# Layer 3 of a four-layer graph kernel: distances once per unordered pair of column blocks, looped by columns

## The chip, the cores and the metric

The kernel runs on one core of a Trainium2 chip. A core has five engines with a queue each, all in order: TensorE (PE in the profile, its weight loads PEld), VectorE (DVE), ScalarE (ACT), GpSimd (POOL) and SyncE (SP, which here issues the transfers). They meet only at semaphores. SBUF is the working memory with 128 partitions; PSUM takes TensorE's results. The metric is the device time of one execution in microseconds; the median of several runs is compared.

## The reference

3327 nodes with 64 features, a dense adjacency matrix of 3327 x 3327 with about 0.2% of its entries set, four layers. Each is `x = x + layer(relu(layernorm(x)), adj)`: two gated graph convolutions, a hyperbolic convolution, a convolution with weights by rank, and the layer that is changed here, a hyperbolic attention:

```python
x_tan = _logmap0(x, C)
left = x_tan @ att_W[:D] + att_b
right = x_tan @ att_W[D:]
adj_att = jax.nn.sigmoid(left + right.T) * adj
x_local = _logmap(x[:, None, :], x[None, :, :], C)
support_t = jnp.einsum('ij,ijd->id', adj_att, x_local)
return _proj(_expmap(x, support_t, C), C)
```

For each pair of nodes (i, j), `_logmap` needs a distance of the two and a factor that depends on this distance alone. Distance and factor are the same for (i, j) and (j, i). The attention is not: sigmoid(left_i + right_j) and adj[i, j] belong to the ordered pair. The sum over j gives, for each i, 64 features and one more number.

## The kernel before, in words

The nodes are padded to 3328 = 26 blocks of 128. Blocks b and b + 13 form a *column*, so there are 13 columns with two halves each. Columns 0 to 5 are group 0 (`gs_`, 768 node columns per half), columns 6 to 12 group 1 (`gf`, 896). Targets i lie along the free axis, sources j on the partitions. A program written in Python emits the instructions; `manual_schedule` leaves them in the order in which they are emitted, so that order is each engine's queue. `Weave` holds generators of other work; each `weave.tick()` emits the next step of those that are due.

Layers 0 to 2 stream the adjacency matrix several times. Layer 3 begins at about 455 us. Its nodes' own quantities come from `nodes3`: for group 1 during layer 2, for group 0 (`gen_s`) woven into layer 3's first steps. It yields some 25 times, with layer norm, transposes, bf16 rows of per-node terms (`rows_i`, `rows_j`), and `leftb`, the left terms spread over all partitions.

The loop before runs over 26 `pairs`: target group 1 with all 13 source columns, then target group 0 with all 13. Step n does for a source column c, with its halves b and the targets' halves k:

- `distances` (L1239, L1251): four products of 64 rows in fp32 and four in bf16 for each k, into PSUM `pair(0)` for b = 0 and `pair(1)` for b = 1. A Gelu (L1259) out of each stands for the logarithm-like factor, a long Tanh (L1266) for the sigmoid.
- `squares` (L1282, L1283 on ScalarE, L1284 on VectorE): the Gelu's result is squared with an offset.
- `weights` (L1294): (tanh + 1) times an adjacency tile, on VectorE.
- `products3` (L1303): (square + HD) times this weight, on VectorE.
- `gather` (L1315): for each half, 64 feature rows accumulated in PSUM banks 2 and 3, the two target halves in the two column halves of the array. `gather_p` (L1332): one more row, with 32-column weights `p2c` whose first column is filled, four products side by side, in bank 0.

Three steps are in work at a time: products of n, attention of n + 1, first distances of n + 2. Tiles of the adjacency come through `Stream`: four slots in layer 3, a load as soon as a slot is free, SyncE's queue (L287), one tile of 128 x 1792 or 128 x 1536 for each half of each step, 52 in all.

After step 12, `collected` for group 1 evicts the accumulators, transposes them, and runs `finish` (L1143 to L1216: some forty small and eight large VectorE instructions, two square roots' worth of table loads on ScalarE, the store); it is woven into the next steps. After step 25 the same follows for group 0 with nothing beside it. A general path behind a branch (`ok < 1`) isn't taken with these inputs.

Of the kernel before, what the change touches and what calls it, by code (L numbers as in the profile page):

```python
# [124 lines left out]

def uses_of_tiles():

    last_first = [2 * c + h for c in reversed(range(HB)) for h in range(2)]
    layer3 = [(g, k) for g in (1, 0) for k in F_SRC + S_SRC]
    starts, uses = [], []  # L130
    for u in (
        FIRST + SECOND + THIRD + LAYER1,
        [(1, k) for k in last_first],
        [(0, k) for k in last_first],
        layer3,
    ):
        starts.append(len(uses))
        uses += u
    return uses, starts[1:]
# [70 lines left out]
def gnn_kernel(ctx: ExitStack, tc: tile.TileContext, t, out):  # L210
# [51 lines left out]
    loaded = [0]  # L262

# [17 lines left out]
    def load_tile(s, key):  # L281
        sum_edges(stream.slots[s][1])
        g, k = key
        pool = slots_a if s < SLOTS3 else slots_b if s < SLOTS2 else slots_c
        a = pool.tile([P, WIDE], F32, name="adj", tag=f"adj{s}")
        a = a[:, : 2 * GROUPS[g].w]
        nc.sync.dma_start(a, t[f"adj{g}"][k * P : (k + 1) * P, :])  # L287
        loaded[0] += 1
        if loaded[0] in between:
            between[loaded[0]]()  # L290
        return a
# [29 lines left out]
    diff = p0.tile([P, P], I32, name="diff")  # L321
    G.iota(diff, pattern=[[1, P]], base=0, channel_multiplier=-1)
    eye, tri, rest, identb = (p0.tile([P, P], BF16, name=n) for n in ("eye", "tri", "rest", "identb"))
# [525 lines left out]

    def by_halves(a):  # L850
        return a.rearrange("p (c a) -> p a c", a=2)

    def nodes3(g, m_t):
# [110 lines left out]
        V.tensor_scalar(p2c[:, sl, 0], qv, 2.0, 2.0, op0=OP.mult, op1=OP.add)  # L964
# [17 lines left out]
    with ExitStack() as c2:  # L982
# [10 lines left out]
        def mask(n):  # L993

            if n < len(work):
                a = stream.tile(stream.now)
                w = 2 * GROUPS[work[n][0]].w
                masks[n] = mk.tile([P, WIDE], BF16, name="mask", tag=f"mask{n % 5}")
# [76 lines left out]
        for n in range(WL):  # L1075
            weights(n)
        for n in range(2):
# [5 lines left out]
        for n in range(len(work)):  # L1083
# [25 lines left out]
            p2c = n3f.tile([P, NB, 32], F32, name="p2c")  # L1109
# [110 lines left out]
    with ExitStack() as cf:  # L1220
        wk = cf.enter_context(right("wkf"))

        pairs = [(i, c) for i in (1, 0) for s in (gf, gs_) for c in s.cs]
        gl, ths, adjs, acc = {}, {}, {}, {}

        def begin(n):
            gl[n] = [wk.tile([P, WIDE], F32, name="gl", tag=f"gl{b}", bufs=3) for b in range(2)]
            ths[n] = [wk.tile([P, WIDE], F32, name="th", tag=f"th{b}", bufs=2) for b in range(2)]

        def distances(n, k):  # L1230

            i, c = pairs[n]
            g = GROUPS[i]
            pts = [pair(b) for b in range(2)]
            for lo, hi in g.chunks:
                for b in range(2):
                    rs = slice(b * D, (b + 1) * D)
                    rhs = (xs, xw)[(k + b) % 2]
                    T.matmul(  # L1239
                        pts[b][:, P + lo : P + hi],  # L1240
                        lhsT=xs[rs, c * P : (c + 1) * P],
                        rhs=rhs[rs, g.c0 * P + lo : g.c0 * P + hi],
                        start=True,
                        stop=False,
                    )
                s = gf if c >= gf.c0 else gs_
                for b in range(2):
                    rs = slice(b * D, (b + 1) * D)
                    j0 = s.off + b * s.w + (c - s.c0) * P
                    i0 = g.off + k * g.w  # L1250
                    T.matmul(  # L1251
                        pts[b][:, P + lo : P + hi],
                        lhsT=rows_j[rs, j0 : j0 + P],
                        rhs=rows_i[rs, i0 + lo : i0 + hi],
                        start=False,
                        stop=True,
                    )
            for b in range(2):
                S.activation(  # L1259
                    gl[n][b][:, k * g.w : (k + 1) * g.w],  # L1260
                    pts[b][:, P : P + g.w],
                    AF.Gelu,
                    scale=-HA,
                )
            kk = 2 * c + k
            S.activation(  # L1266
                ths[n][k][:, : 2 * g.w],
                leftb[:, g.off : g.off + 2 * g.w],
                AF.Tanh,
                bias=righth[:, kk : kk + 1],  # L1270
# [3 lines left out]
        def split(g):  # L1274

            return g.w // 2 + 64, 2 * g.w

        def squares(n):

            m, w = split(GROUPS[pairs[n][0]])  # L1280
            a, b = gl[n]
            S.activation(a[:, :w], a[:, :w], AF.Square, bias=hg)  # L1282
            S.activation(b[:, :m], b[:, :m], AF.Square, bias=hg)  # L1283
            V.scalar_tensor_tensor(  # L1284
                b[:, m:w], b[:, m:w], 2 * HG, b[:, m:w], op0=OP.add, op1=OP.mult
            )

        def weights(n):

            i, c = pairs[n]  # L1290
            for b in range(2):
                a = stream.tile(stream.now)
                th = ths[n][b][:, : 2 * GROUPS[i].w]
                V.scalar_tensor_tensor(th, th, 1.0, a, op0=OP.add, op1=OP.mult)  # L1294
                stream.done()

        def products3(n):

            m, w = split(GROUPS[pairs[n][0]])
            th = ths.pop(n)  # L1300
            for b, lo, hi, hd in ((0, 0, w, HD), (1, 0, m, HD), (1, m, w, HD + HG * HG)):
                a = gl[n][b][:, lo:hi]
                V.scalar_tensor_tensor(a, a, hd, th[b][:, lo:hi], op0=OP.add, op1=OP.mult)  # L1303

        def gather(n):
            i, c = pairs[n]
            g = GROUPS[i]
            if n % HB == 0:
                acc["x"] = accumulators((2, 3))
                acc["p"] = bank(0)  # L1310
            for b in range(2):
                first, last = n % HB == 0 and b == 0, n % HB == HB - 1 and b == 1
                for q, (lo, hi) in enumerate(g.chunks):
                    for k in range(2):
                        T.matmul(  # L1315
                            acc["x"][q][k * D : (k + 1) * D, : hi - lo],
                            lhsT=xd[:, 2 * c + b, :],
                            rhs=gl[n][b][:, k * g.w + lo : k * g.w + hi],
                            start=first,
                            stop=last,  # L1320
                        )

        def gather_p(n):
            i, c = pairs[n]
            g = GROUPS[i]
            a = gl.pop(n)
            for b in range(2):
                first, last = n % HB == 0 and b == 0, n % HB == HB - 1 and b == 1
                for q, (lo, hi) in enumerate(g.chunks):
                    for k in range(2):  # L1330
                        r = 32 * (2 * q + k)
                        T.matmul(  # L1332
                            acc["p"][r : r + 32, : hi - lo],
                            lhsT=p2c[:, 2 * c + b, :],
                            rhs=a[b][:, k * g.w + lo : k * g.w + hi],
                            start=first,
                            stop=last,
                        )

        def evict(g):  # L1340
            m, pp = flat(big(g, "h_n")), flat(big(g, "xc"))
            for q, (lo, hi) in enumerate(g.chunks):
                if q:
                    S.activation(m[:, lo:hi], acc["x"][q][:, : hi - lo], AF.Copy)
                else:
                    V.tensor_copy(m[:, lo:hi], acc["x"][q][:, : hi - lo])
            m0, m1 = (hi - lo for lo, hi in g.chunks)
            V.tensor_copy(pp[:, :m0], acc["p"][:, :m0])
            if m1 > m0:
                S.activation(pp[D:, m0:m1], acc["p"][D:, m0:m1], AF.Copy)  # L1350
            return m, pp

        def collected(g, m, pp):
            yield
            n0, n1 = ((hi - lo) // P for lo, hi in g.chunks)
            ((p, _, _),) = pieces(1)
            for i in range(n1):
                r = 0 if i < n0 else D
                T.transpose(
                    p[:, i * P + r : (i + 1) * P],  # L1360
                    pp[r:, i * P : (i + 1) * P],
                    ident[r:, r:],
                )

            v = p[:, : n1 * P].rearrange("p (i q a r) -> p i q a r", q=2, a=2, r=32)
            for q, n in enumerate((n0, n1)):
                sl = slice(2 * q * n0, 2 * q * n0 + 2 * n)
                V.tensor_mul(
                    sums[:, g.slots, D][:, sl].rearrange("p (i a) -> p i a", a=2),
                    v[:, :n, q, :, 0],  # L1370
                    qs[:, g.slots][:, sl].rearrange("p (i a) -> p i a", a=2),
                )
# [21 lines left out]
        final = None  # L1394


        for n in range(-2, len(pairs)):
# [305 lines left out]
```

## Time and profile before

| | us |
|---|---|
| median of 3 runs | 762.37 (760.78 to 762.52) |
| the profiled execution | 764.75 |
| its span, first to last instruction | 762.9 |
| mean granted TensorE clock in it | 0.950 |
| TensorE busy (share of the span) | 651.7 (85%) |
| VectorE busy | 500.2 (66%) |
| ScalarE busy | 420.7 (55%) |
| GpSimd busy | 5.8 (1%) |
| layer 3's loop, first Gelu to last gather | 455.5 to 740.8 |

The profile is one execution, taken by the hardware profiler. A group's row gives line, engine, operation, tiles, shapes and count, then its busy time, the mean duration of one, and the idle time of its engine just before. The timeline gives start, duration, engine, line and count of neighbouring instructions of one kind; the duration of several is from the first's start to the last's end. Durations overlap where an engine works as a pipeline, so the price of one in a series is the distance between starts. Table rows by stage give the busy time of each engine in a window, then the clock granted to TensorE (1.00 is full), the share of DMA engines in use, and GB/s. The ends of TensorE's products are modelled.

### The profile page before, as it was taken

To read this page: it belongs to the slowest core of one execution; us is meant where nothing else is said; L and a number is where in the kernel's file an instruction comes from. 1 tells how busy PE (TensorE), PEld (TensorE's weight loads), DVE (VectorE), ACT (ScalarE), POOL (GpSimd) and SP (SyncE) were. 2 spreads that over 40 slices of the span, in tenths; PEclk is the share of its full clock that TensorE was granted. 3 is DMA by queue.
4 is the path that set the end of the run, shared out by engine and by line. 5 is a ranking of instruction groups with operands and counts; after the bars stand their busy time and mean duration, and the time that the engine had idled before them with its cause. 6 is when DMAs were issued, how large, how long until landed. Compare 5 with 4: busy or idle time off the path is not lost. (4 is left out here: it accounts for less than half of the span.)

```text
span 762.9 us, 10892 instructions
## 1 busy us (share of the span) xinstructions
PE 651.7 (85%) x4427; PEld 310.9 (41%) x4427; DVE 500.2 (66%) x782; ACT 420.7 (55%) x489; POOL 5.8 (1%) x11
## 2 busy tenths in 40 slices
PE   4988998899779988689979983969999985899970
PEld 2433442343324322458856651423434432344430
DVE  3405764435868015874495436778999978999976
ACT  3203001302554021688867879668999966699941
POOL 0000000000000000000020000000000000000000
PEclk9999999999999999999999996889999998999995
DMA  9999994599958999989477822243555442365400
GB/s 345 413 410 417 342 357 203 169 379 417 414 231 356 417 415 417 375 283 370 155 248 255 299 80 86 97 156 134 193 194 194 166 166 82 137 211 174 166 1 24
DMA packets 33033, 189.73 MB, mean 249 GB/s; under 512 B 3664, under 2 KB 4304, under 8 KB 32976
## 3 DMA queue, kind: packets, MB, share of 16 engines
q1 hardware_dynamic: 32976, 188.97, 65.4%
q8 instruction: 36, 0.59, 0.3%
q14 instruction: 21, 0.17, 0.1%
HBM read 188.10 MB, written 0.85 MB: 248 GB/s over the span
## 5 line engine op out<-in xcount | busy, mean ns | idle before, releaser
L522 PE MATMUL bank<-adj,m_a 128*64 128x384 f32 (+1 forms) x832 | 158.3, 522 | 10.6 <-DMA adj<-in_adj 10.6
L1239 PE MATMUL pair<-xw,xs 64*128 64x384 f32 x208 | 101.3, 569 | 13.5 <-ACT gl L1259 13.5
L1038 ACT ACTIVATE w<-pair,ebias 128x896 uint16<-128x896 f32 (+1 forms) x104 | 96.2, 951 | 19.7 <-PE pair L1030 18.4
L1294 DVE SCALAR_TENSOR_TENSOR th<-th,adj 128x1792 f32<-128x1792 f32 (+1 forms) x52 | 97.6, 1890 | 8.4 <-ACT th L1266 7.9
L1239 PE MATMUL pair<-xs 64*128 64x384 f32 x208 | 101.5, 570 | 0.8 <-ACT gl L1259 0.8
L1259 ACT ACTIVATE gl<-pair 128x896 f32<-128x896 f32 (+1 forms) x104 | 84.0, 862 | 25.9 <-PE pair L1251 25.8
L1303 DVE SCALAR_TENSOR_TENSOR gl<-gl,th 128x1792 f32<-128x1792 f32 (+5 forms) x78 | 97.5, 1304 | 0.4 <-issue 0.4
L522 PEld LDWEIGHTS bank<-adj,m_a 128*64 128x64 f32 x832 | 56.1, 137 | 100.7 <-issue 67.6
L1315 PE MATMUL bank<-gl,xd 128*64 128x384 f32 (+1 forms) x416 | 86.5, 552 | 10.0 <-DVE gl L1303 8.8
L1266 ACT ACTIVATE th<-leftb,righth 128x1792 f32<-128x1792 f32 (+1 forms) x52 | 87.7, 1686 | 0.0
L522 PE MATMUL bank<-adj,m_b 128*64 128x384 f32 (+1 forms) x416 | 78.5, 524 | 2.0 <-ACT hm L611 1.4
L999 DVE TENSOR_SCALAR mask<-adj 128x1792 bf16<-128x1792 f32 (+1 forms) x52 | 53.6, 1053 | 27.2 <-PE pair L1030 27.2
L274 DVE SCALAR_TENSOR_TENSOR edges<-adj,edges 128x1792 bf16<-128x1792 f32 (+1 forms) x24 | 45.0, 1890 | 35.6 <-DMA adj<-in_adj 35.5
L611 ACT ACTIVATE hm<-bank 64x384 f32<-64x384 f32 (+1 forms) x8 | 4.1, 512 | 104.3 <-DVE mh L610 104.1
L1056 PE MATMUL bank<-w,m_b 128*64 128x384 bf16 (+1 forms) x416 | 61.1, 342 | 0.0
L1315 PEld LDWEIGHTS bank<-gl,xd 128*64 128x64 f32 x416 | 32.6, 144 | 58.3 <-issue 29.8
L1251 PE MATMUL pair<-rows_i,rows_j 64*128 64x384 bf16 x208 | 49.5, 350 | 0.0
L1239 PEld LDWEIGHTS pair<-xw,xs 64*128 64x128 f32 x208 | 35.8, 198 | 33.0 <-ACT gl L1259 30.3
L522 PEld LDWEIGHTS bank<-adj,m_b 128*64 128x64 f32 x416 | 29.1, 139 | 47.9 <-issue 42.7
L1239 PEld LDWEIGHTS pair<-xs 64*128 64x128 f32 x208 | 36.0, 199 | 28.0 <-issue 17.5
L1332 PE MATMUL bank<-gl,p2c 128*32 128x384 f32 (+1 forms) x416 | 45.5, 530 | 0.0
L1030 PE MATMUL pair<-mask,tri_b 128*64 128x384 bf16 x208 | 41.7, 347 | 4.5 <-DVE mask L999 4.5
(284 smaller groups left out, 766.3 us busy)
## 6 DMA issues: line engine op xcount, KB each, us to landing
adj<-in_adj SPq DMA_DIRECT2D x104, 896.0 KB, 7.6
adj<-in_adj SPq DMA_DIRECT2D x116, 768.0 KB, 6.8
xn<-in_x SPq DMA_DIRECT2D x3, 192.0 KB, 5.3
w_l<-in_w_l SPq DMA_DIRECT2D x1, 460.0 KB, 9.8
out<-h_n SPq DMA_DIRECT2D x1, 448.0 KB, 4.2
out<-h_n SPq DMA_DIRECT2D x1, 384.0 KB, 2.7
xn<-in_x SPq DMA_DIRECT2D x1, 256.0 KB, 6.9
w_all<-in_w_all SPq DMA_DIRECT2D x1, 67.5 KB, 12.7
```

The source lines that it names most:

```text
L522: T.matmul(acc[q][h * D : (h + 1) * D, : hi - lo], lhsT=m[:, k, :], rhs=a[:, h * g.w + lo : h * g.w + hi], start=first, stop=last,)
L999: V.tensor_scalar(masks[n][:, :w], a, 0.0, None, op0=OP.not_equal)
L1038: S.activation(ws[n][:, h * g.w : (h + 1) * g.w], cnt[h][:, P : P + g.w], AF.Relu, bias=ebias, scale=-EXP_UNIT,)
L1056: T.matmul(acc2[i][q][h * D : (h + 1) * D, : hi - lo], lhsT=p[:, 2 * c + a, :], rhs=ws[n][:, h * g.w + lo : h * g.w + hi].bitcast(BF16), s ...
L1239: T.matmul(pts[b][:, P + lo : P + hi], lhsT=xs[rs, c * P : (c + 1) * P], rhs=rhs[rs, g.c0 * P + lo : g.c0 * P + hi], start=True, stop=False,)
L1251: T.matmul(pts[b][:, P + lo : P + hi], lhsT=rows_j[rs, j0 : j0 + P], rhs=rows_i[rs, i0 + lo : i0 + hi], start=False, stop=True,)
L1259: S.activation(gl[n][b][:, k * g.w : (k + 1) * g.w], pts[b][:, P : P + g.w], AF.Gelu, scale=-HA,)
L1266: S.activation(ths[n][k][:, : 2 * g.w], leftb[:, g.off : g.off + 2 * g.w], AF.Tanh, bias=righth[:, kk : kk + 1], scale=0.5,)
L1294: V.scalar_tensor_tensor(th, th, 1.0, a, op0=OP.add, op1=OP.mult)
L1303: V.scalar_tensor_tensor(a, a, hd, th[b][:, lo:hi], op0=OP.add, op1=OP.mult)
L1315: T.matmul(acc["x"][q][k * D : (k + 1) * D, : hi - lo], lhsT=xd[:, 2 * c + b, :], rhs=gl[n][b][:, k * g.w + lo : k * g.w + hi], start=firs ...
L1332: T.matmul(acc["p"][r : r + 32, : hi - lo], lhsT=p2c[:, 2 * c + b, :], rhs=a[b][:, k * g.w + lo : k * g.w + hi], start=first, stop=last,)
```

## The change

Layer 3's loop now runs over 19 steps m, in three phases. Each has a column c, target columns `tgt` and *turned* source columns `src`:

- phase 1, m = 0 to 6: column 12 down to 6, targets from c up to 12, sources the same without c;
- phase 2, m = 7 to 12: columns 0 to 5 of group 0, targets and sources all seven columns of group 1;
- phase 3, m = 13 to 18: columns 0 to 5, targets from c up to 5, sources the same without c.

For each half b of the column, distances, Gelu and squares are computed once, with c as the source and `tgt` as targets: 91 of the 169 column pairs. The direct direction multiplies them by its attention (`dirs`). For the other direction, in which the columns of `src` are sources and c is the target, TensorE transposes the 128 x 128 squares into PSUM (`turned`), and VectorE multiplies them by the attention of that direction (`trs`), which needs a Tanh of its own for each source block, 256 columns at a time (`tanh_t`). Sums of both directions are added to accumulators that are cleared at first by VectorE: banks 2 and 3 for group 1's features, bank 1 and half of bank 0 for group 0's, and bank 0 for the single rows of all columns, with one of 32 weight columns for each column pair.

All distances use PSUM `pair(0)`, in pieces of up to four target columns, all transposes `pair(1)`. Squares are ScalarE's alone. The adjacency for layer 3 comes from an array of its own, `adj3`, laid out by the host in the order of use: 72 pieces of 256 to 1792 columns. To make room, three tables of layer 0 and 2 move to a pool that closes earlier, and the fifth mask tile of layer 2 is given its place earlier. The steps of the woven generators are spread over six ticks a step.

```diff
+PHASES = [(c, COLS[1][i:], COLS[1][i + 1 :]) for i, c in reversed(list(enumerate(COLS[1])))]
+PHASES += [(c, COLS[1], COLS[1]) for c in COLS[0]]
+PHASES += [(c, COLS[0][i:], COLS[0][i + 1 :]) for i, c in enumerate(COLS[0])]
+def pieces3():
+    for m, (c, tgt, src) in enumerate(PHASES):
+        for half in range(2):
+            if src:
+                yield m, half, True, len(src) * 2 * P
+            yield m, half, False, len(tgt) * 2 * P
...
-    layer3 = [(g, k) for g in (1, 0) for k in F_SRC + S_SRC]
+    layer3 = [p[:3] for p in pieces3()]
...
+        if len(key) > 2:
+            o, w = places[key]
+            src = t["adj3"][:, o : o + w]
...
+        def distances(m, b, i):
...
+            p = pts[m, b, i] = pair(0)
+            for k in range(2):
+                rs = slice(k * D, (k + 1) * D)
+                T.matmul(
+                    p[:, k * 512 : k * 512 + n],
+                    lhsT=(xs if k == b else xw)[rs, c * P : (c + 1) * P],
+                    rhs=xs[rs, ca * P : ca * P + n],
+                    start=True,
+                    stop=False,
+                )
...
+        def gelus(m, b, i):
...
+            S.activation(
+                columns(sqs[m, b], len(tgt))[:, :, lo * P : hi * P],
+                p[:, :, : (hi - lo) * P],
+                AF.Gelu,
+                scale=-HA,
+            )
+        def square(m, b):
+            a = sqs[m, b][:, : 2 * len(PHASES[m][1]) * P]
+            S.activation(a, a, AF.Square, bias=hg)
...
+        def tanh_t(m, k):
...
+            for i, j in enumerate(src):
+                S.activation(
+                    a[:, i * 2 * P : (i + 1) * 2 * P].rearrange("p (b c) -> p b c", b=2),
+                    lb[:, :, o : o + P],
+                    AF.Tanh,
+                    bias=righth[:, 2 * j + k : 2 * j + k + 1],
+                    scale=0.5,
+                )
+        def attention(a, w):
+            V.scalar_tensor_tensor(a[:, :w], a[:, :w], 1.0, stream.tile(stream.now), op0=OP.add, op1=OP.mult)
+            stream.done()
...
+        def factors_d(m, b):
+            n = 2 * len(PHASES[m][1]) * P
+            a = dirs[m, b][:, :n]
+            V.scalar_tensor_tensor(a, sqs[m, b][:, :n], HD, a, op0=OP.add, op1=OP.mult)
+        def turned(m, k, u):
+            c, tgt, src = PHASES[m]
+            cs = src[4 * u : 4 * u + 4]
...
+            p = pts[m, k, "t"] = pair(1)
+            for i, j in enumerate(cs):
+                for b in range(2):
+                    o = (j - tgt[0]) * P
+                    T.transpose(
+                        p[:, (2 * i + b) * P : (2 * i + b + 1) * P],
+                        columns(sqs[m, b], len(tgt))[:, k, o : o + P],
+                        ident,
+                    )
+        def factors_t(m, k, u):
...
+                V.scalar_tensor_tensor(a, pts.pop((m, k, "t"))[:, :n], HD, a, op0=OP.add, op1=OP.mult)
...
+        def gather_t(m, k):
+            c, _, src = PHASES[m]
+            p, o = place(c)
+            for i, j in enumerate(src):
+                for b in range(2):
+                    add(
+                        p[b * D : (b + 1) * D, o : o + P],
+                        xd[:, 2 * j + k, :],
+                        trs[m, k][:, (2 * i + b) * P : (2 * i + b + 1) * P],
+                    )
...
+        for m in range(-1, n_all + 1):
+            old, now, new = m - 1, m, m + 1
+            o, n, f = have(old), have(now), have(new)
+            if n:
+                turned(now, 0, 0)
+            if f:
+                gelus(new, 0, 0)
+            if n:
+                attention_t(now, 0)
+                factors_t(now, 0, 0)
+            weave.tick()
+            if f:
+                begin(new, 0, 1)
+                tanh_d(new, 0)
+            if o:
+                gather_d(old, 1)
+                gather_t(old, 1)
+            if n:
+                attention_d(now, 0)
+                turned(now, 0, 1)
+            if o:
+                singles(old, 1)
...
+            if f:
+                gelus(new, 0, 1)
+                square(new, 0)
+            weave.tick()
+            if n:
+                factors_t(now, 0, 1)
+                factors_d(now, 0)
+                turned(now, 1, 0)
+                gather_t(now, 0)
+                gather_d(now, 0)
+            begin(new, 1, 0)
+            if f:
+                gelus(new, 1, 0)
+                tanh_d(new, 1)
+            weave.tick()
+            if n:
+                attention_t(now, 1)
+                factors_t(now, 1, 0)
+                turned(now, 1, 1)
+            begin(new, 1, 1)
+            if n:
+                singles(now, 0)
+            if n:
+                attention_d(now, 1)
+            if f:
+                gelus(new, 1, 1)
+                square(new, 1)
+            weave.tick()
+            if n:
+                factors_t(now, 1, 1)
+                factors_d(now, 1)
+            if f:
+                tanh_t(new, 0)
+                tanh_t(new, 1)
+            begin(new + 1, 0, 0)
```

Here `begin` calls `distances` (and, ahead of the first column of group 0, waits for `gen_s` and clears bank 1); `tanh_d` is the long Tanh of the direct direction, one for each half; `attention_d` and `attention_t` call `attention` for the two directions; `gather_d` adds the direct products, in runs of up to 512 columns; `singles` adds the single rows of both. Three tiles hold the turned products, four each the squares and the direct ones.

## The prediction

> **What bounds the kernel now.** I read the table of stages first, then the timeline of the layer 3 loop engine by engine, and last the clock around its gaps. A "unit" below is one pair of 128-column blocks with both their halves, 4 squares of 128 x 128; layer 3 has 13 x 13 = 169 units. The page's chain of waits, shares by engine:
>
> ```profile
> PE 10%; DVE 4%; issue 1%; ACT 0%; DVEq 0%
> ```
>
> Stages (window, us, busy of PE, PEld, DVE, ACT, POOL, granted clock, DMA share, GB/s):
>
> ```profile
> 560.00:580.00 20.00, 20.00 (x120) 8.46 (x120) 19.87 (x14) 19.25 (x18) 0.00 (x0) 1.00 0.54 198
> ...
> 640.00:660.00 20.00, 13.86 (x68) 6.64 (x68) 17.41 (x43) 14.81 (x17) 0.00 (x0) 0.76 0.27 93
> ...
> 680.00:700.00 20.00, 20.00 (x146) 9.06 (x142) 19.48 (x15) 19.30 (x21) 0.00 (x0) 1.00 0.55 185
> ```
>
> In the steady parts all three compute engines are full at once: each waits for nothing, so the period is set by sums of work. DMA is half used. VectorE's products (L1303) give the period, in the half with 7 target blocks and in the half with 6:
>
> ```profile
> 594.76 4.02 DVE L1303 SCALAR_TENSOR_TENSOR gl<-gl,th 128x1792 f32<-128x1792 f32 x3
> 604.13 4.02 DVE L1303 SCALAR_TENSOR_TENSOR gl<-gl,th 128x1792 f32<-128x1792 f32 x3
> ...
> 708.42 3.49 DVE L1303 SCALAR_TENSOR_TENSOR gl<-gl,th 128x1536 f32<-128x1536 f32 x3
> 716.63 3.49 DVE L1303 SCALAR_TENSOR_TENSOR gl<-gl,th 128x1536 f32<-128x1536 f32 x3
> ```
>
> 9.37 us for 7 units (other pairs 9.32) and 8.21 for 6: 1.35 us a unit, 13 x 9.32 + 13 x 8.21 = 228 us. From the first Gelu (455.5) to the last gather (740.8) the loop takes 285.3. The other 57 are the node preparation woven into the first four steps (453.66 to 521.84 against 4 x 9.32: 31), the end of the first group woven into four steps (612.61 to 667.43 against 4 x 8.21: 22), and 4 of fill and drain.
>
> **Prices.** ScalarE, start to start:
>
> ```profile
> 598.96 1.79 ACT L1266 ACTIVATE th<-leftb,righth 128x1792 f32<-128x1792 f32 x1
> 600.65 1.78 ACT L1282 ACTIVATE gl<-gl,hg 128x1792 f32<-128x1792 f32 x1
> 602.33 0.72 ACT L1283 ACTIVATE gl<-gl,hg 128x512 f32<-128x512 f32 x1
> 602.94 1.51 ACT L1259 ACTIVATE gl<-pair 128x768 f32<-128x768 f32 x2
> ```
>
> 1.68 for 1792 columns and 0.61 for 512: 0.83 ns a column and 0.19 us for each instruction out of SBUF. Gelus out of PSUM go every 0.70 (768) and 0.80 (896): fixed part 0.06. VectorE: 3.94 for the three products of 3584 columns and 1.40 for 1280 alone: 0.27 us per 256 columns and 0.07 each; reading PSUM costs no more (L1375, 768 columns, 0.96, as L1154 out of SBUF). TensorE:
>
> ```profile
> 281.18 0.98 PE L408 MATMUL pair<-ident,m_t 128*128 128x128 f32 x7
> ...
> 335.82 1.51 PE L763 MATMUL bank<-w,xc 128*64 128x64 f32 x46
> ...
> 666.28 1.50 PE L1332 MATMUL bank<-gl,p2c 128*32 128x384 f32 x16
> ...
> 669.75 2.80 PE L1315 MATMUL bank<-gl,xd 128*64 128x384 f32 x16
> ```
>
> Gathers (L1315) 2.73 to the next start for 6 units: 0.455 a unit; the single-row sums (L1332) 1.43: 0.238. Distances (L1239, L1251) 0.65 + 0.16 for 3 half units, 0.84 + 0.16 for the first after other work. A transpose is 0.27 alone, but seven take 0.98: (0.98 - 0.27) / 6 = 0.12.
>
> **The change, part by part.**
>
> *Removed:* 78 of 169 units of distances, Gelu and square: in work about 78 x 0.55 = 43 us of TensorE, 78 x 0.425 = 33 of Gelu; VectorE's share of the squares (L1284), 13 x (1.40 + 1.20) = 34, goes over to ScalarE.
>
> *Added:* 312 transposes (0.12 each, 37 us); 156 Tanh of 256 columns in place of parts of long ones: 0.19 + 0.21 = 0.40 each. The trace has none of that size. Below, 0.21 without the fixed part; above, the whole 0.72 of the 512-column row; I take 0.40, on the line of two rows. Gathers of 128 columns with weights of their own: L763 runs at 0.029 for each 64-column instruction, the rate of L1315, so 0.23 us for a unit's half stays (above: a 144 ns weight load for each of 4 instructions, 0.58).
>
> *The sums of a middle column* (7 targets, 7 sources, 14 units; six such): TensorE distances 4.5 (two pieces of 1.27 and 1.0 for each half) + transposes 3.4 + gathers 6.4 + single rows 3.3 = 17.6; VectorE 6 x 1.95 + 2 x (1.15 + 0.88) = 15.8; ScalarE Gelu 3.2 + long Tanh 3.4 + squares 3.5 + short Tanh 5.6 = 15.7. Before: 14 x 1.35 = 18.9. By sums the change gains.
>
> *The waits it adds.* Distances have one PSUM pair, transposes the other, where both distance tiles used to alternate. In program order TensorE has distances (new column, half 0, second piece) ahead of the old column's gathers; they wait for the first piece's Gelu, which ScalarE has behind all fourteen short Tanh. Behind them wait the gathers, then the transposes (0,1); for those VectorE's factors; for these the gather of the current column; behind that the distances of half 1; for those ScalarE's Gelu, ahead of the short Tanh of the next turn. That is a ring, once per column:
>
> - ScalarE: Gelu 0.91, Tanh 1.68, Gelu 0.70, square 1.79 (it waits for that Gelu), 14 short Tanh 5.6, next Gelu 0.91: 11.6
> - TensorE: distances 1.0, gather 1.6 + 1.6, six transposes 0.8: 5.0
> - VectorE: factors out of PSUM 0.95, direct factors 2.0: 2.95
> - TensorE: gather 1.6, distances 1.3: 2.9
> - four hand-overs at 0.05 (L408 ends 742.66, L1375 starts 742.69; L1348 ends 741.40, L1359 starts 741.45): 0.2
>
> 22.65 us, above every engine's sum. With 6 sources 0.80 + 0.23 + 0.22 + 0.27 less: 21.1. One unit less in targets and sources takes 3.1 off: 18.0 and 14.9 for 6 and 5 targets. With 4 or fewer there is no second piece, and the ring is Gelu, Tanh, square, half the short Tanh (4.3), four VectorE steps (4.1), gather and distances (2.2): 10.7 with hand-overs, then 8.1, 5.5, 2.8. Sum: 6 x 22.65 + 21.1 + 2 x (18.0 + 14.9 + 27.1) = 277, with 4 of fill 281, against 228 + 4.
>
> *The clock.* The ring leaves TensorE idle for some 5.6 us in a middle column. What 3 us of idleness does now:
>
> ```profile
> 498.00:500.00 2.00, 0.15 (x2) 0.15 (x2) 1.79 (x2) 2.00 (x3) 0.00 (x0) 0.88 1.02 405
> 500.00:502.00 2.00, 2.00 (x16) 1.16 (x18) 0.00 (x0) 1.52 (x2) 0.00 (x0) 0.50 0.95 358
> 502.00:504.00 2.00, 2.00 (x16) 0.65 (x9) 0.00 (x0) 0.00 (x0) 0.00 (x0) 0.77 0.08 32
> ```
>
> 2 us at 0.50 and 2 at 0.77 lose 1.5 us of work, and what comes after the idle time is on the ring. Eleven columns with a second piece: 16; the short columns' TensorE work (5.8 us each way) partly at half clock: 4. I take 20 (none, if the waits are shorter; 28 if all short columns run at half).
>
> *Woven work.* The same steps stay (node preparation in the first columns, the first group's end in the last), VectorE 16 and 17 us of them. The engines now have idle time, so I take 18 + 9 for 31 + 22; bounds 0 and 53.
>
> *At nothing:* the adjacency in pieces. 72 loads for 52, the same bytes, SyncE issues one in 0.33 us; a middle column reads 3.7 MB in 22 us, under the 198 GB/s above, four slots ahead with 4.6 us to land. In the first columns, 14 pieces of 128 to 512 KB, the cover is thin: if gone, 14 x 4.6 less the 27 that these columns last, 37. The PSUM clears (4 of 512, nearest row 0.55 for 384) hide under the node preparation; else 3. Tables of layers 0 to 2 that move to another pool add no instruction there; GpSimd clears 988 columns for 832, long before layer 3. The longer collection after the loop (two small VectorE steps) is under 1.
>
> Sum: 281 + 20 + 27 = 328 for 285.3: +42.7. The span was 762.9, the profiled run 764.75, the median 762.37; on the median 805.
>
> A rule of the Trainium skill, against the trace: TensorE: Matmul & The Clock Gate, Part 4: PE-mode transpose, gives 275 ns for one transpose in a kernel and says that transposes do not count as activity for the clock. The row has 0.27 for one alone and 0.12 in a series. By the page's figure, the six transposes of a ring cost 0.9 us more in eleven columns, some 815 in all (an estimate).
>
> **Rivals.**
>
> *The sums decide* (other side). If the queues run apart enough for the ring to be hidden, TensorE's sum stays: gathers and single rows 169 x 0.693 = 117, distances 91 x 0.55 + 60 pieces x 0.15 = 59, transposes 37; 213, with the 57 of today 270: -15, 747. For it: DVE and ACT sums fall clearly. It decides if a middle column lasts under 18.9. Against: every link of the ring is an in-order queue or a single PSUM pair; to reach 18.9 short Tanh would have to cost 0.13.
>
> *TensorE is the bound through its transposes.* At 0.27 each 312 make 84: 117 + 59 + 84 + 57 = 317, 794. Then TensorE is full, with no wait for Gelu. Against: the series of seven.
>
> *The stream is late at the start:* the price above, 37, gives 842. For: 128 KB pieces are used up in 0.27 us. Against: the node preparation stretches these columns.
>
> **Numbers.** Ring 0.72, TensorE 0.12, late stream 0.08, sums 0.08. Predicted 805. Range: down without the clock loss and with 7 less woven work, 778; up with the woven work at today's 53 and 5 for transposes, 836; the rival by sums and most of the late stream are left out. 0.3% (2.3 us) is what a measurement can tell: faster 0.07 (sums), within 0.02 (between the sums and the ring's low end), slower 0.91.
>
> **What would show it.** Ring: in the middle columns TensorE waits over 4 us a column for the Gelu line, about 22 to 25 us between first Gelus, every engine's busy share under 0.85, clock dips to 0.5 each column, short Tanh 0.40 apart. Wrong if the column lasts under 19, if TensorE is full, or if VectorE waits for DMA.

## The result and the profile after

| | before | after |
|---|---|---|
| median, same chip (range, runs) | 761.58 us (758.79 to 762.52, 4) | 829.71 us (828.62 to 831.21, 4) |
| ratio, 95% interval | | 1.0903 [1.0868, 1.0938] |
| span of the profiled execution | 762.9 | 827.5 |
| mean granted clock | 0.950 | 0.921 |
| busy TensorE, VectorE, ScalarE | 651.7, 500.2, 420.7 | 668.4, 474.8, 405.0 |
| layer 3's loop, first Gelu to end of the last gather | 450.23 to 740.8: 290.6 | 447.98 to 805.5: 357.5 |

The change makes the kernel 9% slower. VectorE and ScalarE have less to do than before and TensorE is busy 17 us more at a lower clock; yet the loop is 67 us longer. The 455.5 that was read as layer 3's first Gelu in the kernel before is its second pair; the first stands 5.3 us earlier:

```profile
450.23 1.73 ACT L1259 ACTIVATE gl<-pair 128x896 f32<-128x896 f32 x2
...
455.51 1.73 ACT L1259 ACTIVATE gl<-pair 128x896 f32<-128x896 f32 x2 [1.88 <-PE pair L1251]
```

In the kernel after, L1318 and L1329 are the distances, L1347 the Gelu, L1356 the square, L1365 and L1384 the long and the short Tanh, L1394 the attention, L1407 and L1429 the direct and the turned factors, L1419 the transposes, L1432 the gathers (`xd`) and single rows (`p2c`).

The stages of the loop, after (window, us, then busy time and instructions of PE, PEld, DVE, ACT, POOL, clock, DMA share, GB/s): columns up to m = 6, the six middle columns, the rest, parted at first Gelus of half 1.

```profile
447.98:564.74 116.76, 85.46 (x727) 47.87 (x728) 69.74 (x102) 78.80 (x112) 0.00 (x0) 0.81 0.39 124
564.74:722.76 158.02, 122.89 (x1259) 74.49 (x1260) 95.41 (x61) 95.12 (x132) 0.00 (x0) 0.87 0.41 138
722.76:806.00 83.24, 65.62 (x693) 39.20 (x693) 63.22 (x107) 46.53 (x74) 0.00 (x0) 0.88 0.32 99
```

Before, three engines were full at once. Now none is: in the middle columns TensorE is busy 78% of the time, partly at half clock, VectorE and ScalarE 60%. A middle column takes 158.02 / 6 = 26.3 us. The waits in that stretch, after (engine, line, what it waited for: us in total, times, longest):

```profile
ACT sq L1347 <- PE pair L1329: 60.4, 11, 10.6
...
DVE tr L1429 <- PE pair L1419: 35.2, 6, 6.6
PE pair L1318 <- ACT sq L1347: 35.1, 12, 5.5
```

The Gelu waits for distances, and the next distances wait for the Gelu: a ring. No wait for a DMA stands in the list, nor in that of the whole loop. ScalarE's half of one turn, in the timeline after:

```profile
617.29 1.02 ACT L1347 ACTIVATE sq<-pair 128x1024 f32<-128x1024 f32 x1 [10.37 <-PE pair L1329]
...
622.42 5.68 ACT L1384 ACTIVATE tr<-leftb,righth 128x256 f32<-128x256 f32 x14
628.00 1.00 ACT L1347 ACTIVATE sq<-pair 128x1024 f32<-128x1024 f32 x1
...
644.33 1.03 ACT L1347 ACTIVATE sq<-pair 128x1024 f32<-128x1024 f32 x1 [10.63 <-PE pair L1329]
```

And TensorE's half, same view:

```profile
629.05 1.00 PE L1318 MATMUL pair<-xs 64*128 64x384 f32 x1 [5.51 <-ACT sq L1347]
...
630.96 3.25 PE L1432 MATMUL bank<-dir,xd 128*64 128x512 f32 x8
634.00 2.34 PE L1432 MATMUL bank<-tr,xd 128*64 128x128 f32 x28
636.26 0.88 PE L1419 MATMUL pair<-ident,sq 128*128 128x128 f32 x6
...
638.74 1.09 PE L1419 MATMUL pair<-ident,sq 128*128 128x128 f32 x8
639.76 1.75 PE L1432 MATMUL bank<-tr,xd 128*64 128x128 f32 x28
641.34 1.67 PE L1432 MATMUL bank<-dir,xd 128*64 128x512 f32 x8
642.94 0.69 PE L1318 MATMUL pair<-xs,xw 64*128 64x512 f32 x1
```

From 617.29 the Gelu of half 1, then Tanh, Gelu, square, fourteen short Tanh 0.40 apart, and at 628.00 the Gelu of the next column's half 0: 10.71 us, in which TensorE runs out of work at 623.5. From 629.05 TensorE is busy without a break until the distances for which the Gelu of half 1 waits (644.33): 15.2 us. The two parts follow each other; hardly anything overlaps them. Twice a direct gather of the same size: 3.04 us to the next start at 630.96 and 1.60 at 641.34. The clock differs (stages of the trace after, 2 us each):

```profile
626.00:628.00 2.00, 0.00 (x0) 0.00 (x0) 1.90 (x2) 2.00 (x6) 0.00 (x0) 1.00 0.00 0
628.00:630.00 2.00, 0.94 (x4) 0.65 (x6) 2.00 (x2) 2.00 (x3) 0.00 (x0) 0.62 0.85 237
630.00:632.00 2.00, 2.00 (x10) 0.44 (x8) 0.62 (x1) 1.59 (x3) 0.00 (x0) 0.50 0.83 280
...
634.00:636.00 2.00, 2.00 (x28) 2.00 (x26) 0.00 (x0) 0.00 (x0) 0.00 (x0) 0.68 0.13 54
636.00:638.00 2.00, 2.00 (x42) 1.66 (x40) 0.82 (x1) 0.00 (x0) 0.00 (x0) 1.00 0.04 8
```

After 5.5 us of idle time the first 6 us of work run at about half clock. Against the same work at full clock the distances (1.9 for 1.0), the direct gather (3.04 for 1.60) and the turned one (2.26 for 1.58) lose 3.0 us.

### The profile page after: what moved, and what is told of

Its sections match the earlier page's. It is cut to its first block, busy times and chain, and to the rows that moved or that the text cites. A ratio compares the mean times of both kernels' runs of the same rounds, so it can differ in the third digit from the quotient of the medians.

```text
span 827.5 us, 13384 instructions
## 1 busy us (share of the span) xinstructions
PE 668.4 (81%) x5592; PEld 360.2 (44%) x5592; DVE 474.8 (57%) x795; ACT 405.0 (49%) x574; POOL 5.9 (1%) x11
## 4 chain that ended last, share of the span: by engine, by line
PE 51%; ACT 17%; DVE 17%; DMA 10%; issue 4%; DVEq 0%; ACTq 0%; SPq 0%
PE bank L558 15%; PE bank L1432 12%; DMA adj<-in_adj 9%; ACT tr L1384 7%; PE pair L1070 6%; PE bank L1096 5%; PE pair L1318 4%; ACT sq L1347 4%; PE pair L659 2%; PE pair L1419 2%; ACT dir L1365 2%; DVE dir L1407 1%; PE pair L463 1%; DVE mask L1039 1%; DVE tr L1394 1%
## 5 line engine op out<-in xcount | busy, mean ns | idle before, releaser
L558 PE MATMUL bank<-adj,m_a 128*64 128x384 f32 (+1 forms) x832 | 158.3, 521 | 11.5 <-DMA adj<-in_adj 11.4
L1347 ACT ACTIVATE sq<-pair 128x1024 f32<-128x1024 f32 (+3 forms) x60 | 48.7, 811 | 121.2 <-PE pair L1329 121.0
L1318 PE MATMUL pair<-xs 64*128 64x512 f32 (+3 forms) x120 | 65.4, 631 | 50.9 <-ACT sq L1347 50.9
L1078 ACT ACTIVATE w<-pair,ebias 128x896 uint16<-128x896 f32 (+1 forms) x104 | 96.4, 952 | 19.5 <-PE pair L1070 18.2
L1429 DVE SCALAR_TENSOR_TENSOR tr<-pair,tr 128x1024 f32<-128x1024 f32 (+3 forms) x52 | 49.7, 956 | 53.6 <-PE pair L1419 50.3
L1432 PE MATMUL bank<-dir,xd 128*64 128x384 f32 (+3 forms) x264 | 61.4, 591 | 17.2 <-DVE dir L1407 17.1
L1394 DVE SCALAR_TENSOR_TENSOR tr<-tr,adj 128x1792 f32<-128x1792 f32 (+6 forms) x34 | 46.8, 1378 | 42.4 <-ACT tr L1384 42.4
L1318 PE MATMUL pair<-xs,xw 64*128 64x512 f32 (+3 forms) x120 | 65.4, 631 | 5.1 <-ACT sq L1347 5.1
L1384 ACT ACTIVATE tr<-leftb,righth 128x256 f32<-128x256 f32 x156 | 63.9, 493 | 0.0
L1407 DVE SCALAR_TENSOR_TENSOR dir<-sq,dir 128x1792 f32<-128x1792 f32 (+6 forms) x38 | 54.4, 1432 | 0.4
L1394 DVE SCALAR_TENSOR_TENSOR dir<-dir,adj 128x1792 f32<-128x1792 f32 (+6 forms) x38 | 54.1, 1424 | 0.0
L1419 PE MATMUL pair<-ident,sq 128*128 128x128 f32 x312 | 47.5, 285 | 5.0 <-DVE tr L1429 3.9
L1356 ACT ACTIVATE sq<-sq,hg 128x1792 f32<-128x1792 f32 (+6 forms) x38 | 49.8, 1312 | 0.7
L1432 PE MATMUL bank<-dir,p2c 128*32 128x256 f32 (+1 forms) x440 | 49.8, 363 | 0.0
L1365 ACT ACTIVATE dir<-leftb,righth 128x1792 f32<-128x1792 f32 (+6 forms) x38 | 49.7, 1307 | 0.0
```

The costliest lines, as they stand in the source:

```text
L558: T.matmul(acc[q][h * D : (h + 1) * D, : hi - lo], lhsT=m[:, k, :], rhs=a[:, h * g.w + lo : h * g.w + hi], start=first, stop=last,)
L1078: S.activation(ws[n][:, h * g.w : (h + 1) * g.w], cnt[h][:, P : P + g.w], AF.Relu, bias=ebias, scale=-EXP_UNIT,)
L1318: T.matmul(p[:, k * 512 : k * 512 + n], lhsT=(xs if k == b else xw)[rs, c * P : (c + 1) * P], rhs=xs[rs, ca * P : ca * P + n], start=True, ...
L1347: S.activation(columns(sqs[m, b], len(tgt))[:, :, lo * P : hi * P], p[:, :, : (hi - lo) * P], AF.Gelu, scale=-HA,)
L1365: S.activation(columns(dirs[m, b], len(tgt)), lb[:, :, o : o + len(tgt) * P], AF.Tanh, bias=righth[:, 2 * c + b : 2 * c + b + 1], scale=0.5,)
L1384: S.activation(a[:, i * 2 * P : (i + 1) * 2 * P].rearrange("p (b c) -> p b c", b=2), lb[:, :, o : o + P], AF.Tanh, bias=righth[:, 2 * j + ...
```

## The experiments

The theory: the order of emission makes a ring of in-order queues, once per column, and the time is its length. The rivals: TensorE is full through the transposes; the low clock is the cause and not a consequence; some engine's sum of work decides. Each ratio is to the kernel before on the same chip; the middle column is taken between Gelus of one kind.

| kernel | median, us (range) | ratio [95%] | middle column |
|---|---|---|---|
| after | 829.71 (828.62 to 831.21) | 1.0903 [1.0868, 1.0938] | 26.3 |
| clock kept up | 806.82 (805.22 to 807.98) | 1.0582 [1.0550, 1.0613] | 23.9 |
| gathers first | 779.60 (779.07 to 781.97) | 1.0235 [1.0203, 1.0267] | 21.3 |
| Gelu first | 786.87 (786.08 to 788.48) | 1.0327 [1.0297, 1.0357] | 21.0 |
| both moves | 791.56 (788.89 to 792.89) | 1.0395 [1.0348, 1.0443] | 21.4 |
| long Tanh | 803.05 (797.49 to 805.37) | 1.0537 [1.0490, 1.0584] | 24.1 |
| no transposes | 806.57 (805.78 to 808.24) | 1.0615 [1.0583, 1.0646] | 24.0 |
| single rows later | 829.84 (828.63 to 830.41) | 1.0897 [1.0867, 1.0927] | 26.9 |
| single rows in the gap | 816.20 (813.49 to 818.78) | 1.0714 [1.0664, 1.0764] | 25.6 |
| reordered | 745.53 (743.12 to 746.77) | 0.9776 [0.9743, 0.9809] | 18.2 |
| reordered, long Tanh | 744.58 (743.11 to 745.31) | 0.9786 [0.9757, 0.9815] | 18.2 |
| reordered, no transposes | 720.36 (719.49 to 722.52) | 0.9483 [0.9452, 0.9514] | 15.65 |

### The clock by itself

```diff
+        def warm(m):
+            for _ in range({5: 10, 6: 15, 7: 20}.get(len(PHASES[m][1]), 0)):
+                add(ps_, idle, rows_i[:, :512])
...
             if f:
+                if n:
+                    warm(new)
                 begin(new, 0, 1)
```

`idle` holds zeros, so the products add nothing.

> Ahead of the second piece of distances of every column with 5, 6 or 7 targets, TensorE gets 10, 15 or 20 products of 512 columns with zero weights that are added to bank 0 (about 0.22 us each); the rest is as in the changed kernel. Theory (a ring through two engines, run in part at half clock): the products lie in TensorE's wait for the Gelu, the clock stays at 1.00, the gathers behind the wait go at full speed, a middle column falls from 26.3 to 23.4 us, the whole by some 25 to 30: 800 to 805. Rival, the clock is not on the path: 829 as before. Rival, TensorE's sum is the bound: 4.4 us more in each middle column, 860.

TensorE's timeline of this kernel (start, us, engine, line):

```profile
614.01 4.48 PE L1432 MATMUL bank<-rows_i,idle 128*128 128x512 bf16 x20
619.69 0.59 PE L1318 MATMUL pair<-xs 64*128 64x384 f32 x1 [1.19 <-ACT sq L1347]
...
620.70 1.72 PE L1432 MATMUL bank<-dir,xd 128*64 128x512 f32 x8
```

With 1.19 us of idle time in place of 5.5 the distances take 1.0 again and the gather 1.55. The granted clock is 1.00 in all middle columns. 23 us come off, 1.8 short of the range expected, and the ring stays: 23.9 us a column at full clock, where TensorE is busy 22.2, 4.5 of them with the zero products, and VectorE and ScalarE 16. The low clock is a consequence of the ring and a third of the loss.

### Opening the ring at one link

Gathers first: TensorE gets the old column's gathers ahead of the second distance piece, which waits for ScalarE.

```diff
+            if o:
+                gather_d(old, 1)
+                gather_t(old, 1)
             if f:
                 begin(new, 0, 1)
                 tanh_d(new, 0)
-            if o:
-                gather_d(old, 1)
-                gather_t(old, 1)
```

> One line moves: the old column's gathers are emitted ahead of the second piece of distances and its wait for the Gelu; same instructions. Theory (ring): 3.2 us of gathers leave the ring, and TensorE's wait shrinks to 2 or 3 us, so that half to all of the clock's loss goes too: a middle column at 20.8 to 22.5 us, the whole at 775 to 800. Rival, a sum of work is the bound (TensorE with its transposes) or the stream of adjacency pieces is late: no change, within 3 us of 829.7.

Gelu first: ScalarE gets the next column's Gelu ahead of the fourteen short Tanh.

```diff
         begin(0, 0, 0)
+        gelus(0, 0, 0)
...
-            if f:
-                gelus(new, 0, 0)
...
+            begin(new + 1, 0, 0)
+            if have(new + 1):
+                gelus(new + 1, 0, 0)
             if f:
                 tanh_t(new, 0)
                 tanh_t(new, 1)
-            begin(new + 1, 0, 0)
```

> The first Gelu of the next column is emitted ahead of the fourteen short Tanh instead of behind them; same instructions. Theory (ring): the next column's second piece of distances no longer waits for the short Tanh; they still stand before the column's first attention. A middle column falls to about 20.5 us plus what the clock still costs (0 to 2), the whole to 775 to 800. Rival, the wait is only where the idle time shows and another limit sits behind it (TensorE's sum, the stream): 820 or more.

Each move alone, with every instruction kept, takes 43 to 50 us off, about 5 us from a middle column. Then both together, at the same two places:

> The changed kernel with both single moves, which alone brought 779.6 (the old column's gathers ahead of the second distance piece) and 786.9 (the next column's first Gelu ahead of the short Tanh). Ring: each opens the same ring at another link and leaves a smaller one, so the gains of 50 and 43 do not add up; the column falls towards TensorE's sum of 17.6 and the time to 745 to 765. Rival, the two gains are of separate waits and add up: 830 - 50 - 43 = 737. Rival, the smaller ring left after the second move (Gelu, first short Tanh, attention and factors on VectorE, gathers, distances) does not hold the moved gathers: 775 to 787, no gain over one move.

Its chain of waits, in order of time (start, us, what), over one column:

```profile
607.06 1.02 ACT sq L1347
608.08 2.79 ACT tr L1384 x7
610.90 2.04 DVE tr L1394
613.03 1.24 DVE tr L1429
614.31 0.88 PE pair L1419 x6
615.19 2.51 PE bank L1432 x32
617.70 1.79 PE pair L1419 x8
619.49 3.18 PE bank L1432 x36
622.67 1.06 PE pair L1318 x4
...
629.12 1.03 ACT sq L1347
```

The gains do not add up, and the 745 to 765 that I expected was a miss: both moves together are slower than the first alone and no faster than the second (the intervals of these two overlap a little). With the Gelu first, the short Tanh of half 0 come late, and another ring closes: Gelu, seven Tanh, attention, turned factors, transposes, single rows, gathers, distances, 22.06 us in the column shown. Two of its links are VectorE's, the 36 gather products on it are the current column's, and the old column's, which were moved, are not: that move has nothing left to gain. The kernel with the Gelu first alone runs on such a ring too: five of its six middle columns take 20.8 us, one 22.06; with both moves it is three and three. The columns of 22 us are those in which the clock dips (0.50 from 616 to 618 in the one shown). I had given this ring as a rival at 775 to 787; it came out worse still.

### The links one by one

Long Tanh: `tanh_t`'s loop over the sources becomes one instruction for a half.

```diff
-            for i, j in enumerate(src):
...
+            S.activation(
+                a[:, : len(src) * 2 * P].rearrange("p (i b c) -> p i b c", b=2, c=P),
+                lb[:, None, :, o : o + P].to_broadcast([P, len(src), 2, P]),
+                AF.Tanh,
+                bias=righth[:, 2 * src[0] + k : 2 * src[0] + k + 1],
...
```

> The changed kernel, but the short Tanh (one for each source block, 0.40 us apart) become one long Tanh for each half: all sources of a half take the first one's right term, so the attention of the turned direction is another. ScalarE then has 2 x 1.68 = 3.4 us in place of 14 x 0.40 = 5.6 in a middle column, 2.3 less; over all columns 156 x 0.40 = 62 becomes 156 x 0.21 + 34 x 0.19 = 39, 23 less. Ring with all short Tanh on it: the middle column goes from 26.3 to about 24.0 and the time from 830 to 805 to 812. Rival, TensorE's sum and clock alone set the column and ScalarE has slack: no change, 830.

No transposes:

```diff
-            p = pts[m, k, "t"] = pair(1)
...
-                    T.transpose(
...
+            pts[m, k, "t"] = sqs[m, k][:, 8 * u * P :]
```

> The changed kernel without the 312 transposes: the turned factors read the squares of one half as they stand in SBUF, so the other direction is summed with wrong squares, by as many VectorE instructions of the same sizes. Ring: of the transposes of a middle column six and then eight stand on it (0.81 + 1.03 us by the trace of the changed kernel), 1.8 less a column, some 26.3 to 24.5, and with the other columns 810 to 815. Rival, the transposes make TensorE the bound: all of them come off, 312 x 0.12 = 37 or more, 793 or below. Rival, they have cover: 830.

26.7 and 23.1 us off, 2 and 3.4 more than the ranges expected: both links stand on the ring. The 2.2 us that a column lost to the long Tanh are what ScalarE saves, though ScalarE sits idle for 10 us at a time: busy share says nothing of a link. Without the transposes the column falls by 2.3 where the two series on the ring are worth 1.8; the other 0.5 was not followed up.

The third link was in doubt. The prediction had VectorE's factors there; the trace shows TensorE busy all through, with the old single rows (1.67) ahead of the transposes of half 1. First they were moved behind the next distances and their Gelu:

```diff
-            if o:
-                singles(old, 1)
...
                 gelus(new, 1, 0)
+            if o:
+                singles(old, 1)
```

> The changed kernel, but the old column's single rows (1.66 us of TensorE in a middle column) are emitted behind the first distance piece of half 1 and its Gelu, not ahead of the transposes (1,0). The prediction's ring has VectorE's factors (2.95 us) as its third link and the single rows beside it: no gain, 828 to 832. Theory after the trace: TensorE is busy without a break from the Gelu of half 0 to the distances of half 1, so its own queue is that link, and 1.66 us come off it until VectorE's 2.95 decides (TensorE's single rows, transposes and gather are 4.3): 1.0 to 1.66 us off each of eleven columns with a second piece, 810 to 819. The long Tanh of half 1 may then wait for the single rows, up to 0.7 us a column, for its tile: that is ScalarE's time behind the Gelu and costs nothing on the ring, or up to 8 in all if it does.

No gain: a miss. From the Gelu of half 0 to that of half 1 the six middle columns took 15.3 us on average for 15.6, but the way back 11.5 for 10.7, since the second distance piece of half 1 now stood behind the single rows. (That makes 0.5 more a middle column; the outer columns gained as much.) And TensorE's timeline shows what is late next:

```profile
634.53 1.09 PE L1419 MATMUL pair<-ident,sq 128*128 128x128 f32 x8 [1.05 <-DVE tr L1429]
```

Now the transposes wait 1.05 us for VectorE's turned factors: with the rows gone, its link shows. So I moved the rows to the idle time, ahead of `begin(new, 0, 1)`:

```diff
+            if o:
+                singles(old, 1)
             if f:
                 begin(new, 0, 1)
...
             if o:
-                singles(old, 1)
```

> The changed kernel, but the old column's single rows are emitted ahead of the second distance piece of half 0, where TensorE now idles 5.5 us in a middle column; in the run before they only moved to another place on the ring (half-0 Gelu to half-1 Gelu 16.33 down to 15.49, half-1 Gelu to half-0 Gelu 10.71 up to 11.61). TensorE's own queue as the third link: half-0 Gelu to half-1 Gelu (first pieces) again about 15.5 or less, now with nothing lost on the other side (10.7), so 0.8 off each of eleven columns, 818 to 823; with the shorter gap the clock may come back too, up to 3 us more a column, then 800 to 818. Rival, VectorE's factors are that link and the single rows have cover: both stretches as in the changed kernel, 830.

13.5 us off. The first stretch fell to 14.9 on average, the way back stayed at 10.7. TensorE is idle 3.85 us at a time for 5.5, still enough for a dip, and the columns alternate: where the clock is low for some 7 us, this stretch takes 15.2 to 15.8, where it is low for half as long, 14.2 to 14.4. So the clock has a part in the gain; what the shorter queue is worth by itself, this run does not tell.

### Another order

All steps stay; a list gives their order within a turn of the loop, with the column that each belongs to. The ticks come six to a turn, as before.

```diff
-        for m in range(-1, n_all + 1):
...
+        order = [
+            ("t",0,0,0), ("gt",-1,1), ("ft",0,0,0), ("td",0,0), ("g",1,0,0), ("ad",0,0), ("sg",-1,1),
+            ("tt",0,1), ("t",0,0,1), ("ft",0,0,1), ("fd",0,0), ("at",0,1), ("p",1,0,1), ("g",1,0,1),
+            ("gd",-1,1), ("td",0,1), ("s",1,0), ("p",1,1,0), ("gd",0,0), ("t",0,1,0), ("ad",0,1),
+            ("fd",0,1), ("g",1,1,0), ("gt",0,0), ("tt",1,0), ("p",1,1,1), ("g",1,1,1), ("sg",0,0),
+            ("ft",0,1,0), ("t",0,1,1), ("ft",0,1,1), ("s",1,1), ("at",1,0), ("p",2,0,0),
+        ]
...
+        for m in range(-3, n_all + 3):
+            for i, (f, d, *a) in enumerate(order):
+                if have(m + d):
+                    emit[f](m + d, *a)
...
```

The letters: `p` distances, `g` Gelu, `s` square, `td` and `tt` long and short Tanh, `ad` and `at` attention, `t` transposes, `fd` and `ft` factors, `gd` and `gt` gathers, `sg` single rows; the first number is the column's offset, then half and piece. The seven short Tanh of a half stand apart (`tt`), and between any two steps that depend on each other, TensorE has other work.

> The same instructions of the 19 columns in another order on all three engines: distances of the next column two pieces ahead, short Tanh of the two halves apart (one between the Gelus of the next column, one behind its squares), single rows and gathers of the old column where TensorE would wait, no step of an engine directly behind a wait for the step before it. Theory (the ring, not the amount of work, is what costs): a middle column lasts what TensorE's sum is, 18 to 19 us, the clock stays at 1.00, the loop takes some 230 to 240 us and the woven work, the whole 735 to 760. Rival, the amount of work (transposes, short Tanh, narrow gathers): 790 or more whatever the order.

16.5 us faster than the kernel before, 84 faster than the change, with as many TensorE products as the change has. Four middle columns in the stages of this kernel (as above):

```profile
559.56:632.45 72.89, 72.89 (x852) 46.07 (x848) 63.86 (x41) 63.39 (x90) 0.00 (x0) 1.00 0.60 203
```

TensorE is full at full clock, none of its products waits for another engine in this stretch, and a column takes 18.2 us. That this is a bound by its sum, and no ring, two more runs show, with the same edits as above:

> The same edit of the Tanh in the reordered kernel (745.5), whose middle column lasts 18.2 us against sums of 17.6 for TensorE and 15.7 for ScalarE. TensorE's sum sets the column: no change, 742 to 748, though ScalarE's work falls by 23. Rival, ScalarE still sets it: up to 23 less, 722 to 728.

> The same removal of the 312 transposes in the reordered kernel (745.5). TensorE's sum sets the column: 1.7 us less work in a middle column, 18.2 to 16.5, where VectorE's 15.8 and ScalarE's 15.7 come close; over all columns 20 to 37 less, 709 to 726. Rival, a ring through ScalarE or VectorE is left that sets the column: under 10 less, 736 to 746.

The long Tanh, worth 27 us in the change's order, is worth nothing here. Without transposes 25 us come off. Four middle columns of that kernel:

```profile
549.79:612.40 62.61, 58.22 (x740) 34.41 (x736) 62.34 (x41) 62.48 (x90) 0.00 (x0) 1.00 0.70 236
```

TensorE's work fell by (72.89 - 58.22) / 4 = 3.67 us a column, 0.131 for each of 28 transposes, but the column by only 2.57: VectorE and ScalarE are full at 15.65. My expectation said 1.7 us of TensorE a column; it had left half the transposes out.

## Why the prediction was right, and where its sizes were off

- **The ring** was right: sign, mechanism and signs to look for. TensorE waits 5.5 us a column for the Gelu line; 26.3 us lie between first Gelus, 24.15 with the clock were forecast; no engine is over 0.85 in the middle columns; and each link that was shortened without lengthening another moved the time.
- **ScalarE's link** fitted: 10.68 without the last Gelu by the prediction, 10.71 in the trace; short Tanh 0.40 apart.
- **The third link was mis-sized.** The prediction put VectorE's factors (2.95) and one gather (1.6) there, 4.55. In the trace TensorE's own queue is longer: single rows 1.67, transposes 1.02, gathers 1.6 and 1.6, 5.87 from 637.07 to 642.94. That is 1.3 a column. With the clock kept up the column took 23.9 for 22.65, the same 1.3. The prediction listed what stood behind the waiting instruction, but did not add up what TensorE had queued beside VectorE's factors: the single rows, the transposes and the first gather are 4.27, more than VectorE's 2.95.
- **The clock was mis-sized in the middle columns**: 1.5 us each by an earlier gap, 3.0 in the column shown, 26.3 - 23.9 = 2.4 on average. In the eleven columns with a second piece the zero products took 23 off where 16 were forecast; the 4 for the short columns no run tests.
- **The sum of the loop**: the middle columns took 158.0 for 144.9 by the prediction's terms (1.3 a column of it the third link, 0.9 the clock); those before 116.8 for 109.6 (rings 81.1, fill 4, clock 6.5, woven 18), those after 82.7 for 74.0 (rings 60, clock 5, woven 9); 29 too little. The 16 us in the outer columns are not settled: the third link is in some of them too, TensorE waits there 17 us for VectorE's direct factors (L1407), and the woven work may have cost more than 27; no run separates these.
- **The base was misread**, and the range was met in part by luck. The prediction took the loop before as 285.3, from 455.5; from the first Gelu at 450.23 it is 290.6. The fill, which was what was left over, is then 9 and not 4. The prediction put the same fill on both sides, so its +42.7 stays if the fill is alike in both kernels, and 5 of the 16 us in the outer columns are fill; no run shows that it is alike. The loop grew by 66.9 and the span by 64.6: layer 3's first Gelu came 2.2 us earlier, and why was not tried. The upper end of the range, 836, stood for woven work at 53 and dearer transposes. The 13 us in the middle columns are of other terms, for which the range left no room; that it was wide enough for them is luck.
- **Rivals.** "The sums decide" falls for this order and is what the reordered kernel does: 18.2 us against a sum of 17.6 for TensorE. The transposes alone don't make the bound (23 us of 68, at 0.13 each). The adjacency was never late: nothing in the loop waits for a DMA.
- **At nothing**: adjacency pieces and clears stayed hidden, as said; the list of waits names neither.

The Trainium skill, TensorE: Matmul & The Clock Gate, HAM oscillation — how this bites in real kernels, says that idle gaps over some 3.4 us bring TensorE back to half clock, with 1.67 us of throttled time for each gap in its kernel. The rows here agree on the first only in part: gaps of 5.5 and 3.85 us gave a dip and 1.19 none, but 2.78 us in the kernel before (ahead of 499.85) gave one too, and 3.44 us ahead of 227.41 in the kernel after gave none. They do not agree on the second: 6 us of slow work after a gap of 5.5. The same page's 275 ns for a transpose (Part 4: PE-mode transpose) does not hold for a series here: 0.131 us each.

## What to carry to other kernels

Less work for every engine is a gain only if the order of the queues lets the engines overlap. For a change of a loop, follow one operand round through all in-order queues until it comes back to its own instruction, and add up everything queued between, that of other columns too; the longest such ring or the fullest engine sets the period. A link is opened by giving the waiting engine something that is ready ahead of the wait, but two good moves can close another ring, as here, so the rings have to be added up anew after each.

## What was not expected of the hardware

A wait of 5.5 us costs TensorE more than the wait: the 6 us of work that follow run at half clock, 3 us lost, and if that work is on the ring, it lengthens the ring. Zero products worth 2.2 to 4.5 us in the gaps of eleven columns brought 23 us in all. And turned gathers of 128 columns, each with its own weights of 64 columns in fp32, cost no more than wide ones: the 28 rows of a half took 1.58 us to the next start, the eight wide direct ones over as many columns 1.60.
